# A two-layer attention kernel over an adjacency matrix: where in the loop the adjacency's byte blocks are made, when the projections' sums are taken, and in what order SyncE issues loads

## The chip, the cores and the metric

The kernel runs on one core of one Trainium2 chip. The metric is the device time of one execution in microseconds (us), given as the median of several runs. One further execution was recorded by the hardware profiler; the traces come from it. The engines are called PE (TensorE, matrix products), DVE (VectorE), ACT (ScalarE), POOL (GpSimd) and SP (SyncE, which here only issues DMAs).

## The reference

`x` is 3327 x 512, `adj` is 3327 x 3327 with zeros and ones (about 1% ones), `W_stack` holds two matrices of 512 x 1024 and `weight` is 512 x 512, all in float32.

```python
def gat_layer(x, W, adj):                      # twice, W = W_stack[0], W_stack[1]
    Wh, Ws = jnp.split(x @ W, 2, axis=-1)
    a = jax.nn.softmax(Wh @ Ws.T, axis=-1) * adj
    return jax.nn.leaky_relu(a @ Wh + x, 0.01)

y = gat_layer(gat_layer(x, W_stack[0], adj), W_stack[1], adj)
x = layernorm(x + y)
ba = jnp.maximum(jnp.sign(x), 0.0)             # zeros and ones
out = jax.nn.relu(adj @ (ba @ jnp.sign(weight).T))
return layernorm(x + out)
```

## The kernel before

**Tiles.** The 3327 rows are 26 row tiles of 128 (the last has 127). Two neighbouring tiles are a pair; there are 13 pairs (NQ). A pair of keys is called q, a pair of queries g; four row tiles are a chunk (7 chunks, the last of two tiles). Nearly every matrix product is done as seven block products instead of eight (the scheme of Strassen and Winograd), so each product needs sums of blocks before it and sums of results behind it. `left_sums` (L179 to L183) and `right_sums` (L185 to L189) are four DVE instructions each, and so their lines L180 to L189 show up in the profile for many tiles; `seven` (L144) is the chain of the seven products with the sums behind them (L162 on DVE, L159 on ACT).

**project(l)** (L233) prepares layer l. It loads the rows of x, transposes them chunk by chunk (`transpose_x`, L245; PE transposes at L253, tile pxt, copied to xT by `copy_out`, L119, which gives odd numbers to ACT and even ones to DVE at L123). `project_values` computes Wh of a pair (tile wh, products at L326) from sums s of xT (`keys`) and of W (`wsum`, L278 to L283), and behind it the sums t of wh (`done`). `queries` computes the other factor: (x M) with M = W_0 W_1^T, its products at L382, from sums of M (`sums_m`, tile msum) and sums xt of xT (`sums` within `queries`); then the sums of its results gsp (`done`) and their stores. Everything goes to memory (xs_d, ws_d, gs_d) for the attention. The loop over the chunks (L417) interleaves by `weave` the queries of chunk c, the values of chunk c and the transposes of chunk c+1. For c > 0 the sums xt of chunk c stand at the head of chunk c's own list (L428), while the sums s stand at the head of its values.

**attention(l)** (L446) is one software pipeline over 169 steps (g, q), g outer. Iteration v (from -34 on) issues, with a position between 0 and 1 for each item and a sort of them (L876), which is the order on each engine:

- loads by SP: ws of step v+2 (three buffers), adj of step v+4 (tile of 128x512, 256 KB, four buffers), xs and gs of scores to come;
- step v+3: `shift` (L620) and `exponential` (L623, ACT);
- step v+2: `running` (sum of the exponentials, L631), `masked` (times adj, L636) and the sums of the masked block on POOL (`sums`, L673 to L676, tiles s and as);
- the scores of a step 30 further on (L477, with copies on ACT and sums on DVE; `maximum`, L547). There are none left when v passes 151. Once per chunk `column_max` folds the maxima (L571) and transposes them (L579);
- the value products of step v: 14 matmuls at L700 into acc;
- one item of `later`, at 0.7. This is the list that `finish(g)` returns at the end of a row g (13 steps): `norm`, `residual`, and in the last layer also `sign`, `turn` (transposes pbt, L788) and `linear` (L798). `fetch(i)` loads the rows that `residual(i)` adds; it has two buffers for each name.

**Byte blocks.** The last stage multiplies by adj again. For it, each adjacency tile is written once as seven blocks of 128x128 bytes (tile ab, float8) to adj_d. Layer l does so in the steps whose q has the parity of l (`s2[1] % L == l`, L862), from the adj tile that the step has loaded anyway: `halved` (two ACT copies, L644 and L645), `halved_sums` (four DVE instructions, L655), `exact` (L664, which tests that the tile holds only zeros and ones, and ends the use of the adj tile) and, an iteration later, `keep_blocks` (store by POOL). So layer 0 does 91 tiles and layer 1 does 78, spread evenly over the rows.

**The end.** In layer 0's last iterations `early` has loads, transposes and products for layer 1's W and M. In layer 1 `load_products(v)` (L912) loads xw (the results of `linear`), forms the right sums of xw (`product_sums`, from step 158 on) and loads the byte blocks (`load_aggregate`); `aggregate` (L959) and `finale` (L964) do the last product and the layernorm.

Which engine's order is whose: SP issues its DMAs in the program's order, and an issue that waits holds up all issues behind it. The adj tile of a step in the last column pair (q = 12) or the last row (g = 12) is zeroed first by POOL, as a whole (L602), and SP's load of it waits for that.

The function that decides which step makes blocks, and the list at the end of a row:

```python
if s2[1] % L == l:
    work += [(-0.1, lambda: halved(*s2)), (0.6, lambda: halved_sums(*s2)),
             (0.62, lambda: exact(*s2))]
    after.append((0.05, lambda s2=s2: keep_blocks(*s2)))
...
fetch(0)
fetch(0)
if not last:
    return [norm, lambda: (residual(0), fetch(1)), lambda: None, lambda: residual(1)]
```

Of the kernel before, what the change touches and what calls it, by code (L numbers as in the profile page):

```python
# [9 lines left out]
F32 = mybir.dt.float32  # L10
# [9 lines left out]
P = 128  # L20
CT = 4
CW = CT * P
HW = CW // 2
# [6 lines left out]
def kernel(  # L30
# [8 lines left out]
    nc = tc.nc  # L39
    N, D = x.shape  # L40
    L = w_stack.shape[0]
# [7 lines left out]
    def rows(t):  # L49
        return min(P, N - t * P)  # L50
# [68 lines left out]
    def copy_out(n, dst, src):  # L119
        if n % 2:  # L120
            nc.scalar.copy(dst, src)
        else:
            nc.vector.tensor_copy(dst, src)  # L123
# [74 lines left out]
            do()  # L198

    ch_lane, acc_lane, tr_lane = (ps_ch, "ch"), (ps_acc, "acc"), (ps_tr, "tr")  # L200
    w_rows, wT, m_of = {}, {}, {}

    def load_w(l, h):

# [4 lines left out]
    def transpose_w(l, h, k, lane):  # L209
        pool, tag = lane  # L210
        pt = pool.tile([P, D], F32, tag=tag, name=f"pwT_{l}_{h}_{k}")
        for d in range(KD):
            nc.tensor.transpose(pt[:, ts(d, P)], w_rows[l, h, d][:, ts(k, P)], ident)
        wT[l, h, k] = slot([P, D], F32, f"wTs_{l}_{h}_{k}")
        copy_out(k, wT[l, h, k], pt)

    def product_m(l, lane):

# [14 lines left out]
    def project(l, pre):  # L233
# [11 lines left out]
        def transpose_x(c, k, lane):  # L245
            if k == 0:
                xTs[c] = pre.tile([P, KD, CW], F32, tag="xT", bufs=2, name=f"xT_{l}_{c}")
            pool, tag = lane
            pt = pool.tile([P, CW], F32, tag=tag, name=f"pxt_{l}_{c}_{k}")
            w = 0  # L250
            for a, t in enumerate(tiles_of(c)):
                r = rows(t)
                nc.tensor.transpose(  # L253
                    pt[:, w : w + r], rows_of[c][a][:r, ts(k, P)], ident[:r, :r]
                )
                w += r
            copy_out(k, xTs[c][:, k, :w], pt[:, :w])
            n = len(tiles_of(c)) * P
            if w < n:
                nc.gpsimd.memset(xTs[c][:, k, w:n], 0.0)  # L260
# [13 lines left out]
        if l == 0:  # L274
            for h in range(2):
                for k in range(KD):
                    transpose_w(l, h, k, (acc_lane, ch_lane)[h])
        wsum = ops.tile([P, 4, 2, HD], F32, tag="gs", name=f"wsum_{l}")  # L278
        lo, hi = wa[:, 0:2], wa[:, 2:4]
        right_sums(  # L280
            lo[:, :, :HD], lo[:, :, HD:], hi[:, :, :HD], hi[:, :, HD:],
            *(wsum[:, i] for i in range(4)),
        )  # L283
        wr = {B11: lo[:, :, :HD], B21: hi[:, :, :HD], B22: hi[:, :, HD:]}
        wr.update({i: wsum[:, e] for e, i in enumerate((T1, T2, T3, T4))})
        m = pre.tile([P, KD, D], F32, tag="m", bufs=1, name=f"m_{l}")
# [117 lines left out]
                for e in range(2):  # L404
                    nc.scalar.copy(m[:, 2 * e : 2 * e + 2], m_of[l][e])

        begin, *chains = queries(0, (ch_lane, acc_lane))
        if l == 0:
            first, second = (project_values(0, a, ch_lane) for a in range(2))
            weave(product_m(l, acc_lane), first + second, [begin])  # L410
            sums_m()
        else:
            first, second = (
                project_values(0, a, lane) for a, lane in enumerate((ch_lane, acc_lane))
            )
            weave(first, second, [sums_m, begin])
        for c in range(NC):  # L417
            turns = []
            if c + 1 < NC:
                turns = [lambda k=k: transpose_x(c + 1, k, tr_lane) for k in range(KD)]  # L420
            if c + 2 < NC:
                load_x(c + 2)
            if c == 0:
                weave(*chains, turns)
            else:
                start, one, two = queries(c, (ch_lane, ch_lane))
                if start:
                    one.insert(0, start)  # L428
                pairs = []
                for a in range(len(tiles_of(c)) // 2):  # L430
                    pairs += project_values(c, a, acc_lane)
                weave(one + two, pairs, turns)
# [13 lines left out]
    def attention(l, att):  # L446
# [150 lines left out]
        def load_adj(g, q):  # L597
            i0, n = half_cols(g)
            at = att.tile([P, 2, HW], F32, tag="adj", bufs=4, name=f"adj_{l}_{g}_{q}")
            adj[g, q] = at  # L600
            if n < HW or rows(2 * q + 1) < P:
                nc.gpsimd.memset(at, 0.0)  # L602
            if rows(2 * q + 1) == P:
                nc.sync.dma_start(
                    out=at[:, :, :n],
                    in_=adjT[2 * q * P : (2 * q + 2) * P, i0 : i0 + n].rearrange(
                        "(a p) i -> p a i", p=P
                    ),
                )
# [126 lines left out]
        def finish(g):  # L736
# [71 lines left out]
            fetch(0)  # L808
            fetch(0)
            if not last:  # L810
                return [norm, lambda: (residual(0), fetch(1)), lambda: None, lambda: residual(1)]
            return [
                norm, lambda: (residual(0), fetch(1)), lambda: sign(0), lambda: turn(0),
                lambda: linear(0), lambda: residual(1), lambda: sign(1), lambda: turn(1),
                lambda: linear(1),
            ]
# [1 line left out]
        if last:  # L818
            binary_weights()
        else:  # L820

            end = len(ahead) - LOOK
            early = {}
            for h in range(2):
                early[end - 14 + 2 * h] = [(0.9, lambda h=h: load_w(l + 1, h))]
                for k in range(KD):
                    early[end - 6 + KD * h + k] = [
                        (0.75, lambda h=h, k=k: transpose_w(l + 1, h, k, tr_lane))
                    ]
# [12 lines left out]
        later, after = [], []  # L842
        for v in range(-LOOK - 4, len(steps)):
            u = v + LOOK

            if 0 <= v + WS - 1 < len(steps):
                load_ws(*steps[v + WS - 1])
            if 0 <= v + 4 < len(steps):
                load_adj(*steps[v + 4])
            for lead, load in ((2, load_xs), (4, load_gs)):  # L850
                if 0 <= u + lead < len(ahead):
                    c, q, h = ahead[u + lead]
                    if h == 0 and (lead == 2 or q == 0):
                        load(c, q)
            work, after = after, []
            if 0 <= v + 3 < len(steps):
                s3 = steps[v + 3]
                work += [(0.0, lambda: shift(*s3)), (0.12, lambda: exponential(*s3))]
            if 0 <= v + 2 < len(steps):
                s2 = steps[v + 2]  # L860
                work += [(0.01, lambda: running(*s2)), (0.4, lambda: masked(*s2))]
                if s2[1] % L == l:  # L862
                    work += [
                        (-0.1, lambda: halved(*s2)), (0.6, lambda: halved_sums(*s2)),
                        (0.62, lambda: exact(*s2)),
                    ]
                    after.append((0.05, lambda s2=s2: keep_blocks(*s2)))
# [12 lines left out]
            if last:  # L880
                load_products(v)
# [30 lines left out]
    def load_products(v):  # L912
# [11 lines left out]
        for t in range(2 * NQ - 2):  # L924
            g, i = divmod(t, 2)
            made = (g + 1) * NQ - 1 + (5, 9)[i]
            if v == max(made + 1, first[t // XH] + t % XH):
                nc.sync.dma_start(out=xw[t], in_=xw_d[t])
        p = v - NQ * (NQ - 1) - 2
        if 0 <= p < EARLY:  # L930
            product_sums(p)
        if v == NQ * NQ - 1:
            product_sums(EARLY)
        n = v - NQ * NQ + 3 * NS
        if 0 <= n < 3 * NS:
            load_aggregate(*divmod(n, NS))
# [27 lines left out]
    def finale(att):  # L964
# [183 lines left out]
```

## Time and profile before

| what | value |
| --- | --- |
| median of 3 runs | 2673.2 us (2670.78 to 2673.9) |
| profiled execution, whole | 2675.18 us |
| its span (first to last instruction) | 2673.3 us |
| PE clock granted, mean | 0.996 of full |
| busy in the span | PE 98%, PE weight load 85%, DVE 78%, POOL 42%, ACT 30% |
| moved by DMA | 635.22 MB, mean 238 GB/s |
| steady row of 13 steps | 79.2 us (layer 0), 81.6 us (layer 1) |
| layer 0 to layer 1: last value product, first step of layer 1 | 1256.8 us, 1532.4 us |
| last row of layer 1 | 2463.9 to 2526.3 us |

A matmul of 128x128 by 128x256 follows the one before it every 0.216 us when nothing is late, though its row in the profile shows some 0.38 us for one, as they overlap in the pipeline. Rows of the timeline have the start, the length, the engine, the line, the operation with its output and inputs, the count, and in square brackets the idle time before it with what ended that. In the list of waits a line has the waiting engine, tile and line, the one waited for, and then the time in total, the number of times and the longest. "L700 PE ... acc" are the value products of the attention, "L477" the scores, "L326" and "L382" the projections, "L959" the last stage.

### The profile page before, as it was taken

How to read it: one execution, taken by the hardware profiler on the slowest of the kernel's cores; microseconds unless marked ns; L12 is line 12 of the kernel's file. 1: busy time of each engine (PE TensorE's matmuls, PEld its weight loads, DVE VectorE, ACT ScalarE, POOL GpSimd, SP SyncE). 2: the span in 40 equal slices, each digit the busy share in tenths (PEclk: the TensorE clock that was granted, in tenths of full speed). 3: DMA queues.
4: the chain of work that ended last, by engine and by line, in shares of the span. 5: the costliest groups of instructions: out<-in, count | busy, mean ns of one | idle time of the engine just before them, and what ended most of it. 6: DMA issues, size and time to landing. Idle time of an engine off the chain costs nothing. (4 is left out here: it accounts for less than half of the span.)

```text
span 2673.3 us, 40191 instructions
## 1 busy us (share of the span) xinstructions
PE 2621.3 (98%) x12839; PEld 2274.0 (85%) x12864; DVE 2075.2 (78%) x4227; ACT 797.9 (30%) x1976; POOL 1127.0 (42%) x2010
## 2 busy tenths in 40 slices
PE   9999999999999999999999999999999999999898
PEld 7888888888888888887888888888888888888687
DVE  5664788788888878888664578888888788889976
ACT  2333322222222222222332323232333323322142
POOL 2550344444444444657453044444444444456510
PEclk9999999999999999999999999999999999999999
DMA  5754767677776766877755667777777777687874
GB/s 195 262 205 155 249 230 258 229 255 236 263 236 230 256 226 234 274 251 232 272 201 190 216 208 267 244 239 248 243 267 238 248 253 237 235 275 264 268 247 167
DMA packets 276536, 635.22 MB, mean 238 GB/s; under 512 B 31809, under 2 KB 133031, under 8 KB 274782
## 3 DMA queue, kind: packets, MB, share of 16 engines
q1 hardware_dynamic: 240558, 526.13, 58.9%
q0 software_dynamic: 35760, 106.45, 11.0%
q8 instruction: 105, 1.72, 0.3%
q14 instruction: 113, 0.93, 0.1%
HBM read 525.52 MB, written 106.93 MB: 237 GB/s over the span
## 5 line engine op out<-in xcount | busy, mean ns | idle before, releaser
L477 PE MATMUL pZ<-gs,xs 128*128 128x256 f32 x2496 | 635.6, 379 | 0.0
L673 POOL TENSOR_TENSOR as<-s 128x128 f32<-128x128 f32 x338 | 159.4, 472 | 1008.7 <-DVE s L636 613.0
L477 PEld LDWEIGHTS pZ<-gs,xs 128*128 128x128 f32 x2496 | 473.7, 190 | 64.5
L700 PE MATMUL acc<-ws,s 128*128 128x256 f32 x1352 | 404.0, 380 | 0.0
L700 PE MATMUL acc<-ws,as 128*128 128x256 f32 x1352 | 351.2, 381 | 9.0 <-DMA ws<-ws_d 5.0
L700 PE MATMUL acc<-wh,s 128*128 128x256 f32 x1352 | 356.7, 380 | 0.3 <-DVE s L636 0.3
L477 PE MATMUL pY<-gs,xs 128*128 128x256 f32 x1248 | 320.3, 379 | 0.0
L623 ACT ACTIVATE s<-s 128x512 f32<-128x512 f32 x338 | 213.4, 631 | 294.9 <-DVE s L620 293.1
L700 PEld LDWEIGHTS acc<-ws,as 128*128 128x128 f32 x1352 | 255.4, 190 | 50.8 <-issue 9.6
L700 PEld LDWEIGHTS acc<-wh,s 128*128 128x128 f32 x1352 | 257.7, 191 | 36.1 <-DVE s L636 0.7
L700 PEld LDWEIGHTS acc<-ws,s 128*128 128x128 f32 x1352 | 256.9, 191 | 35.1 <-DVE h L732 0.5
L547 DVE TENSOR_TENSOR top<-top,s 128x512 f32<-128x512 f32 x312 | 225.5, 732 | 55.0 <-ACT s L529 36.6
L477 PEld LDWEIGHTS pY<-gs,xs 128*128 128x128 f32 x1248 | 237.0, 190 | 32.3
L620 DVE TENSOR_TENSOR s<-s,off 128x512 f32<-128x512 f32 x338 | 255.1, 755 | 0.1
L636 DVE TENSOR_TENSOR s<-s,adj 128x512 f32<-128x512 f32 x338 | 235.4, 696 | 8.6
L519 DVE TENSOR_TENSOR s<-p,u 128x256 f32<-128x256 f32 x156 | 67.2, 431 | 221.7 <-ACT u L494 221.7
L494 ACT COPY u<-pZ 128x256 f32<-128x256 f32 x312 | 116.2, 373 | 391.6 <-PE pZ L477 391.3
L631 DVE TENSOR_TENSOR total<-total,s 128x512 f32<-128x512 f32 x312 | 231.8, 743 | 0.0
L674 POOL TENSOR_TENSOR s<-s 128x128 f32<-128x128 f32 x338 | 201.6, 597 | 27.7
L675 POOL TENSOR_TENSOR as<-s 128x128 f32<-128x128 f32 x338 | 199.3, 590 | 26.5
L676 POOL TENSOR_TENSOR as<-s,as 128x128 f32<-128x128 f32 x338 | 193.4, 572 | 26.5
L700 PE MATMUL acc<-wh,as 128*128 128x256 f32 x676 | 203.4, 383 | 0.0
(200 smaller groups left out, 3914.7 us busy)
## 6 DMA issues: line engine op xcount, KB each, us to landing
ws<-ws_d SPq DMA_DIRECT2D x338, 512.0 KB, 3.8
xs<-xs_d SPq DMA_DIRECT2D x182, 512.0 KB, 5.8
adj<-in_adjT_dram SPq DMA_DIRECT2D x288, 256.0 KB, 4.3
xs<-xs_d SPq DMA_DIRECT2D x156, 384.0 KB, 6.3
gs_d<-gsp POOLq DMA_DIRECT2D x88, 256.0 KB, 3.2
gs<-gs_d SPq DMA_DIRECT2D x12, 1792.0 KB, 10.1
adj_d<-ab POOLq DMA_DIRECT2D x169, 112.0 KB, 3.3
ahl<-adj_d SPq DMA_DIRECT2D x78, 224.0 KB, 4.7
```

What stands on the lines that cost most here:

```text
L477: nc.tensor.matmul(ch[bank], xs[c, q, a][:, k], gs[c][:, b, k], start=(start and k == 0), stop=(k == 1), skip_group_check=True,)
L494: nc.scalar.copy(ch[name], ch[bank])
L547: nc.vector.tensor_tensor(top[i], top[i], t, ALU.max)
L620: nc.vector.tensor_tensor(s, s, off[g].to_broadcast([P, 2, HW]), ALU.subtract)
L623: nc.scalar.activation(sc[g, q], sc[g, q], AF.Exp)
L631: nc.vector.tensor_tensor(total[g], total[g], sc[g, q], ALU.add)
L636: nc.vector.tensor_tensor(s, s, adj[g, q], ALU.mult)
L673: nc.gpsimd.tensor_tensor(s3, a11, a21, ALU.subtract)
L674: nc.gpsimd.tensor_tensor(a21, a21, a22, ALU.add)
L675: nc.gpsimd.tensor_tensor(s2, a21, a11, ALU.subtract)
L676: nc.gpsimd.tensor_tensor(s4, a12, s2, ALU.subtract)
L700: nc.tensor.matmul(acc[g][i // 2][:, i % 2], a[i], b[i], start=(q == 0 and i % 2 == 0), stop=(q == NQ - 1), skip_group_check=True,)
```

## The change

Five things are changed.

1. **Byte blocks.** The tiles that belong to steps of the last four rows (step index 117 and up: 28 tiles in layer 0, 24 in layer 1) are made earlier, in steps of index below 117 whose q has the other parity, spread evenly over these ("room"). Such a step loads the late step's adj tile in addition to its own, with the same four buffers, and then does halved, halved_sums, exact and keep_blocks on it. The last four rows make no blocks.
2. **W's sums.** `wsum` of layer 1 is formed by `sums_w` in halves at steps 150 and 151 of layer 0's attention, not in project(1). In layer 0 it is formed at its old place, in halves (eight instructions for four).
3. **Projections.** The copies of pxt to xT for c > 0 are all on ACT. `prepare(c + 1)` makes the sums xt of chunk c+1 as the last item of chunk c's transposes, no longer at the head of chunk c+1's list.
4. **Loads.** `fetch(1)` goes into the next item of `later`. The adj tiles of the last row and column pair are zeroed only where the load leaves them free: the last column, or the second half of the tile. The loads of xw come two steps later.
5. **Sums of xw.** `product_sums(11)`, in the last iteration before, is done in `finale`, just ahead of `product_sums(12)`.

```diff
+    def sums_w(l, k):
+        if k == 0:
+            wsum_of[l] = ops.tile([P, 4, 2, HD], F32, tag="gs", name=f"wsum_{l}")
+        lo, hi = w_rows[l, 0, k], w_rows[l, 0, 2 + k]
+        right_sums(
+            lo[:, :HD], lo[:, HD:], hi[:, :HD], hi[:, HD:],
+            *(wsum_of[l][:, i, k] for i in range(4)),
+        )
...
-            copy_out(k, xTs[c][:, k, :w], pt[:, :w])
+            if c:
+                nc.scalar.copy(xTs[c][:, k, :w], pt[:, :w])
+            else:
+                copy_out(k, xTs[c][:, k, :w], pt[:, :w])
...
-        wsum = ops.tile([P, 4, 2, HD], F32, tag="gs", name=f"wsum_{l}")
+        if l == 0:
+            for k in range(2):
+                sums_w(l, k)
+        wsum = wsum_of[l]
         lo, hi = wa[:, 0:2], wa[:, 2:4]
-        right_sums(
-            lo[:, :, :HD], lo[:, :, HD:], hi[:, :, :HD], hi[:, :, HD:],
-            *(wsum[:, i] for i in range(4)),
-        )
...
+        def prepare(c):
+            start, *chains[c] = queries(c, (ch_lane, ch_lane if c else acc_lane))
+            if start:
+                start()
...
                 turns = [lambda k=k: transpose_x(c + 1, k, tr_lane) for k in range(KD)]
+                turns.append(lambda: prepare(c + 1))
...
-                start, one, two = queries(c, (ch_lane, ch_lane))
-                if start:
-                    one.insert(0, start)
+                one, two = chains[c]
...
-            if n < HW or rows(2 * q + 1) < P:
-                nc.gpsimd.memset(at, 0.0)
+            if n < HW:
+                nc.gpsimd.memset(at[:, :, n:], 0.0)
+            if rows(2 * q + 1) < P:
+                nc.gpsimd.memset(at[:, 1], 0.0)
...
             if not last:
-                return [norm, lambda: (residual(0), fetch(1)), lambda: None, lambda: residual(1)]
+                return [norm, lambda: residual(0), lambda: fetch(1), lambda: None,
+                        lambda: residual(1)]
             return [
-                norm, lambda: (residual(0), fetch(1)), lambda: sign(0), lambda: turn(0),
+                norm, lambda: residual(0), lambda: (sign(0), fetch(1)), lambda: turn(0),
                 lambda: linear(0), lambda: residual(1), lambda: sign(1), lambda: turn(1),
...
+            for k in range(2):
+                early[end - 2 + k].append((0.8, lambda k=k: sums_w(l + 1, k)))
...
+        first = NQ * (NQ - 4)
+        mine = [i for i, e in enumerate(steps) if e[1] % L == l]
+        room = [i for i, e in enumerate(steps[:first]) if e[1] % L != l][2:]
+        late = [i for i in mine if i >= first]
+        blocks = {i: steps[i] for i in mine if i < first}
+        blocks.update(
+            {room[n * len(room) // len(late)]: steps[i] for n, i in enumerate(late)}
+        )
...
                 load_adj(*steps[v + 4])
+                if blocks.get(v + 4, steps[v + 4]) != steps[v + 4]:
+                    load_adj(*blocks[v + 4])
...
-                if s2[1] % L == l:
+                of = blocks.get(v + 2)
+                if of:
...
-            if v == max(made + 1, first[t // XH] + t % XH):
+            if v == max(made + 3, first[t // XH] + t % XH):
...
-        if v == NQ * NQ - 1:
-            product_sums(EARLY)
...
-        product_sums(NQ - 1)
+        for p in range(EARLY, NQ):
+            product_sums(p)
```

More of the change, by code (lines that the diff above doesn't have):

```diff
@@ L200 @@
     ch_lane, acc_lane, tr_lane = (ps_ch, "ch"), (ps_acc, "acc"), (ps_tr, "tr")
-    w_rows, wT, m_of = {}, {}, {}
+    w_rows, wT, m_of, wsum_of = {}, {}, {}, {}
     def load_w(l, h):
@@ L405, in sums_m @@
                     nc.scalar.copy(m[:, 2 * e : 2 * e + 2], m_of[l][e])
-        begin, *chains = queries(0, (ch_lane, acc_lane))
+        chains = {}
+        def prepare(c):
+            start, *chains[c] = queries(c, (ch_lane, ch_lane if c else acc_lane))
+            if start:
+                start()
         if l == 0:
             first, second = (project_values(0, a, ch_lane) for a in range(2))
-            weave(product_m(l, acc_lane), first + second, [begin])
+            weave(product_m(l, acc_lane), first + second, [lambda: prepare(0)])
             sums_m()
@@ L415, in project @@
             )
-            weave(first, second, [sums_m, begin])
+            weave(first, second, [sums_m, lambda: prepare(0)])
         for c in range(NC):
@@ L423, in project @@
             if c == 0:
-                weave(*chains, turns)
+                weave(*chains[c], turns)
             else:
-                start, one, two = queries(c, (ch_lane, ch_lane))
-                if start:
-                    one.insert(0, start)
+                one, two = chains[c]
                 pairs = []
@@ L861, in attention @@
                 work += [(0.01, lambda: running(*s2)), (0.4, lambda: masked(*s2))]
-                if s2[1] % L == l:
+                of = blocks.get(v + 2)
+                if of:
                     work += [
-                        (-0.1, lambda: halved(*s2)), (0.6, lambda: halved_sums(*s2)),
-                        (0.62, lambda: exact(*s2)),
+                        (-0.1, lambda: halved(*of)), (0.6, lambda: halved_sums(*of)),
+                        (0.62, lambda: exact(*of)),
                     ]
-                    after.append((0.05, lambda s2=s2: keep_blocks(*s2)))
+                    after.append((0.05, lambda of=of: keep_blocks(*of)))
             if later:
```

## The prediction

> **What bounds the kernel now.** I read the first lines of the page, then the busy time by stretches of 100 us, then what PE waited for, then single stretches in order of time.
>
> ```profile
> span 2673.3 us, 40191 instructions
> ...
> PE   9999999999999999999999999999999999999898
> ...
> DVE  5664788788888878888664578888888788889976
> ```
>
> PE is busy in 98% of the span, so it sets the end, and only stretches in which it isn't full can give time back. The stretches show where:
>
> ```profile
> 700.00:800.00 100.00, 100.00 (x470) 88.02 (x469) 84.74 (x171) 29.78 (x77) 43.91 (x79) 1.00 0.74 252
> 1200.00:1300.00 100.00, 91.93 (x402) 72.76 (x401) 84.67 (x167) 24.52 (x56) 60.02 (x100) 0.98 0.68 230
> 2400.00:2500.00 100.00, 91.30 (x419) 76.58 (x420) 94.89 (x184) 25.41 (x59) 63.20 (x109) 0.98 0.83 280
> 2500.00:2600.00 100.00, 93.02 (x736) 80.47 (x739) 80.11 (x201) 33.40 (x64) 24.62 (x44) 0.97 0.70 235
> ```
>
> The columns are the stretch, its length, busy time of PE, PE's weight load, DVE, ACT and POOL, PE's clock, the DMA share and GB/s. From 700 to 800 us PE never rests, though DVE is busy in 85%. At the layer boundary (1200 to 1300) and the end of the last attention layer (2400 to 2530) it loses some 8 us per 100, and the clock falls below 1. What it waited for:
>
> ```profile
> PE pbt L788 <- DVE ba L782: 5.1, 1, 5.1
> PE acc L700 <- DMA ws<-ws_d: 5.0, 2, 4.4
> PE pxt L253 <- DVE xT L123: 3.4, 1, 3.4
> PE pZ_g L382 <- ACT h_wh L159: 2.9, 6, 0.5
> PE pZ_wh L326 <- DVE s L181: 2.7, 2, 2.3
> PE acc L700 <- POOL s L674: 2.7, 1, 2.7
> ```
>
> (microseconds in total, times, longest). Each is few and long: they are events, not a steady loss. Three cost more than they show, because PE ran at half clock after them:
>
> ```profile
> 1284.39 0.66 PE L253 MATMUL pxt<-ident,xr 128*128 128x128 f32 x4 [3.37 <-DVE xT L123]
> 1284.89 3.44 PE L382 MATMUL pY_g<-xt,msum 128*128 128x256 f32 x8
> ```
>
> Eight such matmuls took 1.89 us at 1276.91. After the gap of 3.37 they took 3.44; after the gaps of 4.38 (2474.56) and 5.14 (2499.24), pairs took 0.86 instead of 0.43. After gaps of 2.35 (1263.09) and 2.70 (2464.91) nothing slowed. So a gap between 2.70 and 3.37 or above costs about 1.6 to 2.6 us more than its length. [...]
>
> **Part 1: blocks (halved, halved_sums, exact) moved out of the last rows.** A block costs DVE 2.36 us (2444.52 to 2446.88: four L655 of 0.28 to 0.54, one L664 of 0.83, 0.08 for its accumulator), ACT 0.71 and POOL 0.56. The last row of layer 1 lasts 62.4 us (2463.9 to 2526.3). PE's work in it is 41.8: 13 steps of 14 matmuls at 0.216, 3.02 each, plus 2.5 for transposes and finish(11). In the stretches 2489.2 to 2498.6 and 2510.7 to 2521 PE does run 3.02 a step, so that is attainable. The excess of 20.6 is waits (2.70 + 4.38 + 0.59 + 5.14 + 0.33 + 0.79 = 13.9), about 5 of half clock, and small ones. DVE is busy 59.8 of the 62.4. Without five to six blocks (-11.4 measured between 2468.75 and 2521.9, up to -14 for six) and with one product_sums (1.04) gone to the finale, DVE has about 45 left beside PE's 41.8. So DVE, not PE, sets this row: 45 to 48 us. That takes off 14 to 17; I take **-16** for the row with the ws waits of part 4, bounds -12 (ws still late) and -20.6 (PE alone).
>
> In layer 0 the last rows have DVE 0.88 busy and PE waits of 0.63, 0.85 and 0.54 (1190, 1206, 1234) within 3.9 us of excess: **-3** (-1.5 to -4).
>
> What it adds: 28 and 24 blocks in the first nine rows, two to four per row, each between two steps that have blocks of their own, and each with its own load of adj. DVE's steady rows (79.2 us in layer 0, 81.6 in layer 1) hold 64 to 68.2 us; three blocks add 7.1, so the share goes from 0.81-0.84 to 0.90-0.93. Below 1, with about 10 us from a mask product to the matmul that needs it, an extra 2.36 is absorbed. Two covers are thin: the fold L571 ends 0.22 us before its transposes in layer 0's rows (once per two rows), and POOL's sums have 4 to 7 us. If a block falls just before a fold, PE waits up to 2.36. I take **+1.5** (0 to +6, a wait of half a block at five of twelve folds). The loads are 52 x 256 KB, 13.3 MB over 1500 us, 9 GB/s beside 252; a load lands in 4.3 us and is issued four steps (24 us) early, but the same four buffers hold fewer steps ahead; the buffer comes free when the exactness test of the iteration before ends, which leaves about 0.9 of an iteration of 6.1 us. Hidden, at zero; without the cover the step's mask product would wait, inside DVE's 10 us.
>
> [...] In the trace 128x512 sums of two SBUF inputs took 0.68 where POOL ran no sums (L186 to L189, 1261.41 to 1264.4) and 0.69 to 0.76 on average where POOL is busy 0.44. [...]
>
> **Part 2: W's sums earlier (sums_w), copies of xT to ACT, xt sums a chunk sooner (prepare).** At the boundary, PE's wait of 2.35 for s (L181) is DVE being late through the four wsum (L186 to L189, 1261.41 to 1264.4); they go to steps 150 and 151, where DVE has room, so that s is ready 2.4 sooner. But the xt sums behind hang on msum, which stands in DVE's order behind neg_w, whose DMA lands at 1269.9 in either order: most of what is won there is waited again. The gap of 3.37 is the copy L123 at 1283.65, queued on DVE behind t's sums; on ACT (30% busy) it is done when the transposes end. That gives 3.37 and the 1.6 of half clock, and I take 0.8 of the rest: **-5.8** (-4 to -7). Layer 0's start has eight half sums for four whole: **+0.2**.
>
> The chunks behave otherwise. Now, chunk starts 2 to 5 of each layer cost PE 0.48 to 0.69 (the wait for ACT's h_wh), against 0 where nothing is late; from start to start 0.63 more than the matmuls. DVE's order there is t (four, 1.47), s (four), xt (four, 2.53), and PE's first product needs only s. After the change, prepare(c+1) stands at the end of the chunk before, so DVE does xt (2.53) first, then the queries' sums gs (L189 at 1320.59 is the last of four, 2.52), then t (1.47), then s up to L181 (0.87). From the last value sum wb (L162, 0.35 apart from the next): 0.35 + 2.53 + 2.52 + 1.47 + 0.87 = 7.74, and about 0.14 to PE (1265.29 to 1265.44 at the boundary): 7.88. PE's product for wb began 1.06 before that sum (1330.08 and 1331.14); from there to the product that needs s it has eight groups of four matmuls (0.8625 each) and four transposes (0.436): 6.9 + 0.436 - 1.06 = 6.28. It waits 1.60 at L326 where it lost 0.63: 0.97 x 8 = **+7.7**. Bounds: -5 (0.63 x 8) if s comes in time, +10 if ACT's h_wh follows late as well.
>
> **Part 3: loads moved on SyncE.** fetch(1) goes one item later. At 2359.75 PE waits 1.56 for xs, since SP's issue of it stood from 2345.24 to 2352.80 behind fetch(1), which waits for residual(0): **-1.7** (0 to -2). Past it move the ws, adj and xs loads of one iteration; it is itself needed two or three items later, 12 us or more, and lands in 4.
>
> **Part 4: memset only where needed, xw loads two steps later.** In the last row, SP waits:
>
> ```profile
> SPq L604 <- POOL adj L602: 14.7, 7, 3.9
> ...
> SPq L681 <- PE acc L700: 10.3, 8, 3.4
> SPq L115 <- DMA xres<-x_d: 8.2, 3, 3.6
> ```
>
> The 14.7 is adj's load behind POOL's memset, and the ws load behind it is the 4.38 gap. The memset of 128x512 (0.53 x 10) becomes a column or a half tile. The wait goes; next late is the fetch, called twice, on the same queue (8.2), two to four us a time, and ws has three buffers of 3 us. This is inside the -16 above. The xw loads are used by product_sums from step 158 on, and only tiles 22 and 23 come later for it (part 5): zero.
>
> **Part 5: product_sums(11) into the finale.** Its 1.04 now stands before product_sums(12), which PE's wait of 1.2 for L187 shows to be on the path at that point: **+1.0** (0 to +1.1).
>
> **Sum**: -16 - 3 + 1.5 - 5.8 + 0.2 + 7.7 - 1.7 + 1.0 = -16.1. From the profiled execution's 2675.18 that gives 2659.1. That execution lies 2.0 above the median of 2673.2, so **2657 us**.
>
> **Rivals.**
> A (13%, the other side): the first 117 steps pay for the blocks. Mechanism: a block in DVE's queue delays fold, or the mask product before a value step, past PE's need. It decides against the gain from 16.1/52 = 0.31 us per moved block on; at 0.6 each (a quarter of a block) it is +31, less the +1.5 counted: 2657 + 30 = 2687. For: fold's cover of 0.22, DVE to 0.93. Against: no PE wait between 700 and 800 with DVE at 0.85, and 10 us of slack.
> B (18%): the chunk starts don't wait, as the sums in front of s were never late by as much as the order says. Then +7.7 becomes about -3: 2646.
> C (17%): the last row stays bound by ws behind the double fetch, or DVE finds no pace: half the gain, -8: 2665.
> D (5%): the change does not do what it says at all, the waits return elsewhere in the same size: 2670 to 2676.
> My forecast (47%): 2652 to 2662.
>
> **How the numbers follow.** Range 2642 to 2670 takes in the forecast, B, C and a part of D, and leaves out A and tails. Some 0.2% (5.3 us, 2667.9 to 2678.5) is what a measurement of this kernel tells from no change. Faster by more: forecast, B and 0.14 of C, 0.79. Within: D, 0.03 of C and 0.02 of A, 0.10. Slower: the other 0.11 of A.
>
> **What would show it.** Right: the last row (L700 to the first L959) at 45 to 48 us with no half clock in it; no PE wait on xT at the second chunk of layer 1; PE waits of about 1.6 for s (L181's) at the starts of chunks 2 to 5; steady rows still 79.2 and 81.6. Wrong: rows of the first nine that are longer by 1 us or more, with waits of ptop for top or acc for s; chunk starts below 0.6; a last row above 54 us.

## The result, and the profile after

The changed kernel takes **2681.4 us** (median of 10 runs, 2679.74 to 2685.08) against 2672.69 us (10 runs, 2670.78 to 2673.95) before: a ratio of 1.0035 with a 95% interval of 1.0026 to 1.0045. It is slower by a third of a per cent, where 2657 was forecast, with a range of 2642 to 2670. The profiled execution took 2681.87, its span is 2680.1.

The page of the changed kernel has nearly the same first lines:

```profile
span 2680.1 us, 40370 instructions
...
PE   9999999999999999999999999999999999999897
...
DVE  5554888899888996666755488988899888767876
```

DVE's digits are higher in the middle of each attention layer and lower at its end: the blocks were moved as the change says. The stretches of 100 us (columns as before) show where time came and went:

```profile
400.00:500.00 100.00, 95.71 (x436) 83.45 (x435) 85.74 (x183) 29.67 (x79) 39.63 (x78) 0.97 0.72 246
500.00:600.00 100.00, 100.00 (x468) 88.02 (x467) 89.17 (x189) 30.96 (x82) 42.74 (x82) 1.00 0.77 265
...
700.00:800.00 100.00, 96.28 (x438) 83.89 (x437) 85.79 (x184) 29.04 (x78) 39.16 (x77) 0.97 0.73 244
...
1200.00:1300.00 100.00, 96.95 (x435) 77.69 (x434) 73.77 (x132) 24.05 (x47) 55.65 (x102) 1.00 0.69 227
...
2400.00:2500.00 100.00, 94.91 (x447) 81.17 (x449) 72.49 (x121) 22.16 (x43) 56.97 (x104) 1.00 0.81 274
```

The boundary (1200 to 1300) and the end (2400 to 2500) gained, as forecast. These stretches don't hold quite the same work (the last row begins at 2463.9 before and at 2479.7 here); the table further down compares like with like. But PE, which was full from 300 to 1000 us, now loses about 4 us in two of these stretches, with a lowered clock, while the stretch between them, with DVE at 89%, is full. What PE waited for:

```profile
PE pZ_wh L338 <- DVE s L181: 12.3, 9, 1.7
PE pZ L494 <- ACT u L511: 9.7, 5, 4.3
...
PE acc L719 <- DMA ws<-ws_d: 4.6, 3, 3.7
PE agg L992 <- DVE wh L187: 2.0, 2, 1.5
```

Eight of the nine waits in the first line are the chunk starts, forecast at 1.60 each. The second is new and was not forecast: scores (L494) that wait for a copy on ACT (L511). On PE it looks like this, in the seventh step of layer 0's row 1:

```profile
414.23 0.59 PE L719 MATMUL acc<-ws,s 128*128 128x256 f32 x2
419.12 2.08 PE L494 MATMUL pZ<-gs,xs 128*128 128x256 f32 x4 [4.29 <-ACT u L511]
420.99 1.06 PE L719 MATMUL acc<-wh,as 128*128 128x256 f32 x2
```

and on ACT:

```profile
418.20 0.40 ACT L663 CAST ab<-adj 128x256 fp8e4<-128x256 f32 x1 [7.22 <-DMA adj_d<-ab]
418.51 0.29 ACT L664 CAST ab<-adj 128x128 fp8e4<-128x128 f32 x1
418.71 0.36 ACT L511 COPY u<-pZ 128x256 f32<-128x256 f32 x1
```

ACT stood 7.22 us in front of `halved`, the cast into the block tile ab, because ab has two buffers and the store of the block two before (adj_d<-ab) had not landed. Behind it in ACT's order stood the copy u that PE needed. PE's 4.29 is followed by half clock: two matmuls take 1.06 instead of 0.59. POOL had issued that store at 407.05, right behind one of a residual:

```profile
406.50 0.56 POOL L115 DMA_DIRECT2D x_d<-h  x1 [2.84 <-DVE h L786]
407.05 0.54 POOL L677 DMA_DIRECT2D adj_d<-ab  x1
```

It took 11.1 us to land, the longest of the 169 stores of ab:

```profile
DMA to landing us min/median/max: 2.0/3.9/11.1
```

Before, the longest took 7.3, and ACT never waited for one.

The time of a row (13 steps, from its first value matmul to the next row's first, and for a layer's last row to the end of its last value matmul) adds it up:

| stretch, us | before | after | difference | forecast |
| --- | --- | --- | --- | --- |
| rows 0 to 8 of layer 0 | 712.8 | 727.4 | +14.6 (row 1 +7.4, row 5 +7.0) | +1.5 for both layers |
| rows 0 to 8 of layer 1 | 731.6 | 736.1 | +4.5 (rows 1, 4, 5, 8) | (in the line above) |
| rows 9 to 12 of layer 0 | 251.7 | 249.8 | -1.9 | -3 |
| rows 10 and 11 of layer 1 | 124.4 | 122.2 | -2.2 | -1.7 |
| last row of layer 1 | 62.4 | 51.7 | -10.7 | -16 |
| to layer 0's first row | 292.4 | 296.2 | +3.8 | +0.2 and half of +7.7 |
| layer 0's end to layer 1's first row | 275.6 | 272.6 | -3.0 | -5.8 and half of +7.7 |
| behind the last row | 147.0 | 148.7 | +1.7 | +1.0 |

The differences are +6.8 in sum, which is 2680.1 - 2673.3.

### The profile page after: what moved, and what is told of

Its sections match the earlier page's. It is cut to its first block, busy times and chain, and to the rows that moved or that the text cites. A ratio compares the mean times of both kernels' runs of the same rounds, so it can differ in the third digit from the quotient of the medians.

```text
span 2680.1 us, 40370 instructions
## 1 busy us (share of the span) xinstructions
PE 2622.6 (98%) x12839; PEld 2273.6 (85%) x12864; DVE 2059.8 (77%) x4211; ACT 813.0 (30%) x2000; POOL 1093.4 (41%) x2029
## 2 busy tenths in 40 slices
DMA packets 290800, 648.84 MB, mean 242 GB/s; under 512 B 32765, under 2 KB 147295, under 8 KB 289046
## 5 line engine op out<-in xcount | busy, mean ns | idle before, releaser
L494 PE MATMUL pZ<-gs,xs 128*128 128x256 f32 x2496 | 640.3, 381 | 10.9 <-ACT u L511 9.7
L692 POOL TENSOR_TENSOR as<-s 128x128 f32<-128x128 f32 x338 | 163.9, 485 | 1011.1 <-DVE s L655 661.3
L494 PEld LDWEIGHTS pZ<-gs,xs 128*128 128x128 f32 x2496 | 475.1, 191 | 79.6 <-ACT u L511 12.8
L494 PE MATMUL pY<-gs,xs 128*128 128x256 f32 x1248 | 320.3, 379 | 0.0
L494 PEld LDWEIGHTS pY<-gs,xs 128*128 128x128 f32 x1248 | 237.0, 190 | 32.3
L639 DVE TENSOR_TENSOR s<-s,off 128x512 f32<-128x512 f32 x338 | 247.9, 734 | 0.1
L511 ACT COPY u<-pZ 128x256 f32<-128x256 f32 x312 | 116.1, 372 | 328.8 <-PE pZ L494 328.2
L694 POOL TENSOR_TENSOR as<-s 128x128 f32<-128x128 f32 x338 | 205.1, 607 | 26.5
L693 POOL TENSOR_TENSOR s<-s 128x128 f32<-128x128 f32 x338 | 182.2, 539 | 27.7
L695 POOL TENSOR_TENSOR as<-s,as 128x128 f32<-128x128 f32 x338 | 179.4, 531 | 26.5
## 6 DMA issues: line engine op xcount, KB each, us to landing
gs<-gs_d SPq DMA_DIRECT2D x12, 1792.0 KB, 10.5
```

The lines of the kernel that those rows point to most:

```text
L494: nc.tensor.matmul(ch[bank], xs[c, q, a][:, k], gs[c][:, b, k], start=(start and k == 0), stop=(k == 1), skip_group_check=True,)
L511: nc.scalar.copy(ch[name], ch[bank])
L639: nc.vector.tensor_tensor(s, s, off[g].to_broadcast([P, 2, HW]), ALU.subtract)
L692: nc.gpsimd.tensor_tensor(s3, a11, a21, ALU.subtract)
L693: nc.gpsimd.tensor_tensor(a21, a21, a22, ALU.add)
L694: nc.gpsimd.tensor_tensor(s2, a21, a11, ALU.subtract)
```

## The experiments

Eleven kernels. Medians of before in the same sets of runs were 2672.86, 2671.95 and 2673.97 us (first four, next four, last three).

**1. A third buffer for ab in layer 0.**

```diff
-            t = att.tile([P, 7, P], F8, tag="adj_b", bufs=2, name=f"ab_{g}_{q}")
+            t = att.tile([P, 7, P], F8, tag="adj_b", bufs=3 - l, name=f"ab_{g}_{q}")
```

> A third buffer for the byte-block tile ab in layer 0's attention only (there is no room for it in layer 1's, which serves as the control). Theory R (ring): a block in the step between two others leaves the third of three only 0.85 of a step to get its buffer back, and the store of the first lands later than that; ACT waits, and PE behind it. Then rows 1 and 5 of layer 0 go from 86.6 and 86.2 us to 79.2, the half clock after them goes, layer 1's rows stay as in the changed kernel (82.2, 82.9, 82.5 and 83.2 in rows 1, 4, 5 and 8): 2681 - 14.4 = 2667 (2665 to 2669). Theory Q (DVE's queue: the block's 2.36 us of DVE are what is late): nothing moves, 2681. Theory L (the added loads crowd the transfers): nothing moves, 2681.

Measured: 2669.86 us, ratio 0.9987 (0.9978 to 0.9997), just above what was expected. Rows 1 and 5 of layer 0 are 79.2 and 79.3; layer 1's rows 1, 4 and 8 are 82.1, 83.5 and 83.2 still. Row 5 of layer 1 is 81.6, without a change to it, and 81.5 in runs 2 to 5: its 82.5 was seen in the changed kernel's trace alone. ACT's cast no longer waits there:

```profile
411.03 0.37 ACT L511 COPY p<-pY 128x256 f32<-128x256 f32 x1 [1.35 <-PE pY L494]
411.30 0.41 ACT L663 CAST ab<-adj 128x256 fp8e4<-128x256 f32 x1
411.60 0.30 ACT L664 CAST ab<-adj 128x128 fp8e4<-128x128 f32 x1
412.32 0.37 ACT L511 COPY u<-pZ 128x256 f32<-128x256 f32 x1 [0.42 <-PE pZ L494]
```

Theory R holds: with the same blocks on DVE and the same loads, one buffer takes 14.3 us off the rows 0 to 8 of layer 0 (727.4 to 713.1). The stores are no faster, the longest takes 11.3; ACT no longer waits for them. The median falls by 11.5 only, as other stretches of this trace are longer by 1.8 in sum. That alone turns the change from slower to slightly faster than before. That layer 1 has no room for a third buffer was not shown: no run tries it there.

**2. The added loads left out.**

```diff
-                    load_adj(*blocks[v + 4])
+                    adj[blocks[v + 4]] = adj[steps[v + 4]]
```

> The changed kernel without the 52 added loads of adj: a moved block is made from the tile that its step has loaded for itself, so the byte blocks of the moved steps hold other data and the last product is of other numbers; all else is the same. Theory R (ring): the stores still have to land within 0.85 of a step, so rows 1 and 5 of layer 0 stay near 86 us or lose at most a few us of it, 2676 to 2682. Theory L (the added 13.3 MB of loads make the stores late): the waits for ab go in both layers, 2681 - 19 = 2662. Theory Q: unchanged, 2681.

Measured: 2678.4 us, ratio 1.0023 (1.0013 to 1.0032). Rows 1 and 5 stay at 84.7 and 86.5, and ACT waits for ab as before (32.3 us in 12 waits, against 29.9 in 10):

```profile
418.56 1.13 PE L494 MATMUL pZ<-gs,xs 128*128 128x256 f32 x4 [3.56 <-ACT u L511]
```

Theory L falls: the 13.6 MB of added loads (648.84 MB are moved in the changed kernel, 635.21 here) cost at most some 3 us.

**3. Sums s ahead of sums xt.** `prepare(c)` calls `keys` of the chunk's first pair first:

```diff
         def prepare(c):
+            if c:
+                sums_of[c, 0] = keys(c, 0)
             start, *chains[c] = queries(c, (ch_lane, ch_lane if c else acc_lane))
...
```

> The changed kernel, with the sums s of the next chunk's first pair ahead of the sums xt at the end of each chunk (keys, then prepare). Theory O (order of sums on DVE): s is late only because xt, gs and t stand ahead of it, so the eight waits of 1.45 to 1.66 at the starts of chunks 2 to 5 go, and xt is still in time (4.4 us of DVE against 6.3 of PE): 8 x 1.60 = 12.8 less, 2668.5 (2667 to 2671); if the old loss of 0.63 comes back it is 2673.6. Theory C (the xT copies, all four on ACT now, hold the chunk start): the waits stay, 2681.

Measured: 2665.28 us, ratio 0.9964 (0.9952 to 0.9977), in its trace 15.2 us less than the changed kernel (2664.9 against 2680.1). That is more than was expected: the eight waits were 12.0 in sum, and the two projections are 6.8 and 7.0 us shorter. In the changed kernel DVE's order at a chunk start is xt, gs, t and then s:

```profile
1331.10 0.68 DVE L186 TENSOR_TENSOR gsp<-b,gsp 128x512 f32<-128x512 f32 x1
...
1335.55 0.42 DVE L181 TENSOR_TENSOR s<-s,xT 128x256 f32<-128x256 f32 x1
```

and PE's product waits for that s:

```profile
1336.12 1.10 PE L338 MATMUL pZ_wh<-wsum,s 128*128 128x256 f32 x4 [1.45 <-DVE s L181]
```

With keys first the same product (now L340) follows without a gap:

```profile
1326.85 0.60 PE L263 MATMUL pxt<-ident,xr 128*128 128x128 f32 x4
1327.29 1.03 PE L340 MATMUL pZ_wh<-wsum,s 128*128 128x256 f32 x4
```

Theory O holds; neither the 1.60 nor the old 0.63 is left at any of the eight starts.

**4. xt back at the head of its chunk.**

```diff
-                turns.append(lambda: prepare(c + 1))
...
-                one, two = chains[c]
+                start, one, two = queries(c, (ch_lane, ch_lane))
+                if start:
+                    one.insert(0, start)
```

> The changed kernel with the sums xt of each chunk back at the head of its own list, as before; the copies to xT stay on ACT. Theory O: each of the eight chunk starts goes from 1.60 back to about 0.63, or less as the DVE copy of xT is gone: -7.8, 2673.5 (2671 to 2675). Theory C (copies on ACT): the waits stay, 2681.

Measured: 2673.29 us, ratio 0.9997 (0.9987 to 1.0006). The waits of 1.45 to 1.66 are the old ones again (0.47 to 0.69), with the copies to xT still on ACT. Between 80 and 180 us PE waited for:

```profile
PE pZ_g L394 <- ACT h_wh L159: 1.4, 3, 0.5
PE pZ_g L394 <- DVE xt L187: 0.7, 1, 0.7
```

The median is 8.1 us below the changed kernel's (2681.4 - 2673.3). In the trace the two projections give 3.7 and 2.5 of this: in layer 1 PE now waits 2.06 for xt at the boundary, where it waited 0.45. So the loss at the chunk starts comes from the place of `prepare`, and none of it from the copies.

**5. One fetch(0).**

```diff
             fetch(0)
-            fetch(0)
```

> The changed kernel with fetch(0) called once instead of twice. Theory S (SyncE's queue): in the last row of layer 1 the second fetch stands on SP until the first has landed (8.1 us in three waits), the ws loads behind it come late, and that is PE's wait of 3.70 (and 0.37, 0.57) for ws. Then these go and the last row falls from 51.7 to 47 to 48 us: 2677 (2676 to 2678). Theory D (DVE, busy 0.94 of this row, sets it): the wait for ws goes and others for DVE's or POOL's sums take its place, the row stays at 50.5 to 51.7, 2680.5 to 2681.5.

Measured: 2679.06 us, ratio 1.0024 (1.0015 to 1.0034). The wait for ws is gone from the last row, and others took its place. In it PE waited for:

```profile
PE pbt L807 <- DVE ba L801: 4.1, 2, 2.9
PE acc L719 <- POOL as L694: 1.2, 2, 0.8
PE pz L767 <- POOL adj L619: 0.9, 1, 0.9
```

The row is 50.9 instead of 51.7, as theory D said: S falls, D holds for the row. The median lies between the two forecasts, 2.3 us below the changed kernel's; most of the trace's gain is outside the row, in the stretch behind it (146.5 instead of 148.7) and in rows 0 to 8.

**6. Layer 1 without moved blocks at q 4 and 8.**

```diff
-        room = [i for i, e in enumerate(steps[:first]) if e[1] % L != l][2:]
+        room = [i for i, e in enumerate(steps[:first]) if e[1] % L != l and (l == 0 or e[1] not in (4, 8))][2:]
```

> The changed kernel; in layer 1 the moved blocks do not go to steps with q 4 or 8, in layer 0 nothing is different. Theory H: of the blocks that stand third of three, those pay in layer 1 whose first one's store is queued on POOL right behind the 256 KB store of h (residual(0), residual(1)), which are these. Then rows 1, 4, 5 and 8 of layer 1 go from 82.2, 82.9, 82.5 and 83.2 to 81.5 or 81.6: -4.5, 2677 (2676 to 2678), and layer 0's rows 1 and 5 stay near 86. Rival: which store is late is a matter of where the gs loads and others fall, and the waits move to other rows in the same sum, 2681.

Measured: 2681.48 us, ratio 1.0031 (1.002 to 1.0043). ACT's waits for ab are gone from layer 1 (14.9 us in 4, all in layer 0), as theory H said. The time is not: rows 1, 4, 5 and 8 are 82.9, 82.6, 81.5 and 82.6. Two other waits are there. In rows 4 and 8, with a moved block at q 2, PE waits for u (0.66 each; the changed kernel has these two as well, 0.66 and 0.67). In row 4:

```profile
1890.25 1.13 PE L494 MATMUL pZ<-gs,xs 128*128 128x256 f32 x4 [0.66 <-ACT u L511]
```

and ACT had waited for DVE's shift (L639), which stood behind a block, two maxima and a residual:

```profile
1889.31 0.63 ACT L642 ACTIVATE s<-s 128x512 f32<-128x512 f32 x1 [4.87 <-DVE s L639]
1889.85 0.35 ACT L511 COPY u<-pZ 128x256 f32<-128x256 f32 x1
```

In row 1, now with blocks at q 12 and at q 0 of the next row (four in succession), PE waits for xs, whose load SP issued late:

```profile
1695.20 1.10 PE L494 MATMUL pZ<-gs,xs 128*128 128x256 f32 x4 [1.10 <-DMA xs<-xs_d]
```

H named the right waits on ACT, but they held only a part of layer 1's price, and the new places brought the wait for xs. The new theory, that q 2 and the succession 12, 0 cost, is tried in 9.

**7. Blocks not moved, all else of the change kept.**

```diff
-        blocks = {i: steps[i] for i in mine if i < first}
-        blocks.update(
-            {room[n * len(room) // len(late)]: steps[i] for n, i in enumerate(late)}
-        )
+        blocks = {i: steps[i] for i in mine}
```

> The changed kernel with part 1 undone: each layer makes the blocks of its own parity in their own steps, nothing is loaded twice; all the rest of the change stays. Theory B: moving the blocks is what freed DVE in the last rows, so the last row of layer 1 goes from 51.7 back to 59 to 61 us, rows 9 to 11 lose some 2 more, and the rows before them are 79.2 and 81.6 throughout: 2681.4 - 18.9 + 11 = 2673.5 (2671 to 2676). Rival M (the smaller memset alone shortened the last row): it stays near 52, 2664.

Measured: 2676.97 us, ratio 1.0018 (1.0008 to 1.0027), a little above what was expected. All rows 1 to 8 are 79.2 and 81.5 to 81.6; the last row of layer 1 is 61.6, with

```profile
PE pbt L807 <- DVE ba L801: 8.5, 2, 5.6
PE acc L719 <- POOL as L694: 4.3, 4, 2.6
```

So theory B holds: the smaller memset and the fetch bring 0.8 us of the last row (62.4 to 61.6), the moved blocks 9.9 (61.6 to 51.7). What was not expected is row 11 of layer 0 at 66.4, against 63.0 before: there `sums_w` stands on DVE ahead of a fold, and PE waits 2.56 for it; with the blocks moved away it is 0.80.

**8. All repairs.** Third buffer (1), keys first (3), one fetch (5), the room of (6), and

```diff
-        constants()
         for p in range(EARLY, NQ):
             product_sums(p)
+        constants()
```

> All that the theories R, O, S and H ask for: a third buffer of ab in layer 0, keys of the next chunk's first pair ahead of xt, one fetch(0), no moved block at q 4 or 8 of layer 1; and product_sums(11) and (12) before the constants of the last stage instead of behind them. If each of them is right and they add up: 2681.4 - 14 (ab) - 15 (sums) - 4 (fetch) - 4.5 (room) - 1.5 (product sums, which wait 6.67 us for ACT's square root now) = 2642 (2639 to 2647). If the fetch gives nothing (theory D): 2646. If the ring's waits come back elsewhere: 2655 or above.

Measured: 2646.91 us, ratio 0.9905 (0.9889 to 0.9922), near the 2646 of the case in which the fetch gives nothing. The terms of that sum were not as expected: `room` gave nothing in run 6 where 4.5 was put, and the stretch behind the last row is 143.9 instead of 148.7, -4.8 where 1.5 was put; the two misses cancel by luck. The measured parts do add up: by runs 1, 3, 5 and 6 the first four repairs are -11.5, -16.1, -2.3 and +0.1, which with -4.8 makes 2646.8. The -4.8 was not run by itself: that stretch is about 144 in runs 8 to 10, and between 146.5 and 151.0 in the other traces.

**9. The same, layer 1's moved blocks at q 0, 6 and 10 only.**

```diff
-        room = [i for i, e in enumerate(steps[:first]) if e[1] % L != l and (l == 0 or e[1] not in (4, 8))][2:]
+        room = [i for i, e in enumerate(steps[:first]) if e[1] % L != l and (l == 0 or e[1] in (0, 6, 10))][2:]
```

> As the run with all repairs, but layer 1's moved blocks go to q 0, 6 and 10 only. Theory: what is left of part 1's price in layer 1 (83.3, 82.6 and 82.6 in rows 1, 4 and 8, against 81.5 and 81.6) has two causes: a moved block at q 2, whose 2.36 us of DVE stand beside residual's 2.2 and make the exponential late, which stands ahead of a score copy on ACT (0.66 at PE); and blocks at q 12 and then q 0, four in succession, which hold an xs load on SP behind an adj load without a buffer (1.5 at PE). Neither is left then: -3.6, 2643.5 (2642 to 2645). If these waits come with the number of blocks and not with their places, they move, 2647.

Measured: **2643.8 us**, ratio 0.9888 (0.9871 to 0.9904), the fastest version. Rows 1, 4, 5 and 8 of layer 1 are 81.5, 81.6, 81.5 and 81.6: the price of moved blocks in layer 1 was one of places. Which of the places left out (q 2, the succession of 12 and 0) brought how much is read from run 6's waits alone. Its longest waits that are left:

```profile
PE pxt L263 <- DMA xr<-in_x_dram: 5.1, 3, 4.0
PE pbt L811 <- DVE ba L805: 4.2, 2, 2.9
PE acc L723 <- POOL as L698: 2.1, 4, 0.8
```

**10. The repairs of 8, no block moved.** The diffs of 3, 5, 7 and 8's last together.

> As the run with all repairs, but no block is moved (each in its own step, as before). Theory B: moved blocks are worth what the last rows show, 10 in the last row of layer 1 and 2 to 4 in layer 0's, and cost nothing once their waits are gone, so this is 2647 + 9 to 12 = 2656 to 2659. Rival: with the sums, the fetch and the product sums in order, the last row is short in any case, 2647 to 2650.

Measured: 2658.49 us, ratio 0.9943 (0.9926 to 0.9959). The last row is 61.7 again, row 11 of layer 0 65.6. Moving the blocks is worth 14.7 us (2658.5 - 2643.8) once its waits are gone.

**11. The last row without sums of xw.** With one fetch, `product_sums` of the loop is left out and the last product reads columns of xw instead.

```diff
         if 0 <= p < EARLY:
-            product_sums(p)
+            a = min(2 * p % XH, XH - 3)
+            xt[p] = xw_tiles[2 * p // XH][:, a : a + 2].rearrange("p a (b n) -> p (a b) n", n=HD)
```

> The changed kernel with one fetch(0) and without the eleven product_sums of the loop: the last product reads other numbers in their place, so its result is not the sums' product; all else is done. It takes 10 x 1.6 us of DVE out of the last row of layer 1. Theory D (DVE sets the last row): the row goes from 50.9 (run with one fetch) to 43 to 46 us, close to PE's own 41.8, and pbt's waits for ba (4.1) and acc's for POOL's sums go: 2679 - 6 = 2673 (2671 to 2675). Rival (loads or the order of steps set it): it stays at 49 to 51, 2678 to 2679.

Measured: 2674.29 us, ratio 0.9999 (0.999 to 1.0009). The last row falls from 50.9 to 46.3, a little above the expected 43 to 46. The row in the changed kernel and here:

```profile
2479.70:2531.40 51.70, 43.78 (x201) 35.18 (x203) 48.49 (x96) 8.75 (x15) 35.47 (x65) 1.00 0.85 295
```

```profile
2477.80:2524.20 46.40, 42.75 (x201) 35.69 (x203) 37.46 (x57) 8.79 (x15) 35.37 (x65) 1.00 0.91 315
```

DVE's time goes from 48.5 to 37.5, and PE follows: theory D holds for this row. The ten product_sums had taken 16.1; DVE gains less, as what else it does takes 37.5 in the shorter row, with POOL busy 0.76 of it, instead of 48.5 - 16.1 = 32.4 with POOL busy 0.69.

## Why the prediction was wrong

**The step that failed** is the one in part 1 on what the moved blocks add: "Below 1, with about 10 us from a mask product to the matmul that needs it, an extra 2.36 is absorbed", taken at +1.5 with 0 to +6. It measured +19.1 (14.6 + 4.5). As far as it went, it was right: DVE at 0.91 and 0.92 in rows 3 and 4 of layer 0 cost nothing (79.2 and 79.4), and the loads were hidden but for some 3 us at most (run 2). It followed DVE, POOL, the loads and adj's four buffers, but not the other tile that a block goes through, ab, with two buffers that come free only when a store has landed. It even noted the fact that decides, that each moved block lies between two steps with blocks of their own, and drew nothing from it. The third of three needs the buffer of the first within about 0.85 of a step (5.2 us); the stores land in 3.9 us in the median, but in up to 11.1. In the place shown above ACT was ready for the third block at 410.98, 3.9 us behind the issue of the first one's store.

Runs 1 and 2 show that this is layer 0's 14 us. Why the two stores that stopped PE there took 11.1 and 10.5 us stays open: each was issued within 0.8 us behind a 1792 KB load of gs by SP and a store of a residual by POOL, and no run takes these away; without the added loads ACT still waited 6.5 and 6.9. Layer 1's 4.5 is shared: rows 4 and 8 are 82.6 in run 6, without any wait for ab, so that about 2.0 belongs to the late exponential at q 2; the other 2.5 has ACT's waits for ab in front of PE's (0.46, 0.73 and 0.32). Run 9's places avoid both.

**Rival A** ended near the result (2687) by another mechanism. DVE's queue did delay PE, but only at two places of layer 1, by 0.66 each; A's price of 0.6 for each of the 52 blocks was 31 us. That ACT, the least busy engine of the four that compute (30%), could be the one to hold PE was in none of the cases.

**The last row**: -16 was forecast, -10.7 measured, in the same mechanism. The mis-sized term is "DVE has about 45 left": it is 48.5. Of the sum's 59.8 - 11.4 (or 14) - 1.04 the last part was not in this row: before, too, the row held ten product_sums, and the one that went to the finale ran at 2527 to 2529, behind it. And the sums that stayed became longer: the ten product_sums take 16.1 instead of 14.9, a running sum 0.87 instead of 0.75. The wait for ws behind the double fetch was there (3.70), but run 5 shows that it stood in front of DVE's lateness.

**Layer 0's last rows**: -3 against -1.9; the sums of W at steps 150 and 151, costed at nothing, take part of it (row 11 at 66.4 in run 7).

**The chunk starts**: +7.7 forecast, and the waits are 1.45, 1.45, 1.45 and 1.66 in each layer, for old waits of 0.48 to 0.69. From one start to the next it is 27.61 us instead of 26.64: the +0.97 that DVE's order of instructions gave. Runs 3 and 4 show that it was the order alone. Rival B falls.

**The boundary**: -5.8 against -6.9 (-3.0 less the 3.9 of layer 1's chunk starts). PE's 3.37 and the half clock are gone. **SyncE's fetch(1)**: -1.7 against -1.8 (row 10 of layer 1, 66.2 to 64.4). Not all of it is sure to come from there: run 7, which keeps this part, has 65.7, with a wait of 0.99 for xs. **product_sums(11)**: +1.0 against +0.7 in PE's waits for L187 (1.24 to 1.97); the other 1.0 of that stretch lies partly behind the last matmul (13.4 us to the end against 12.8).

Without the failing step and with the right last row the sum is 2675.2 - 10.7 - 1.9 + 7.7 - 6.9 - 2.2 + 1.7 = 2662.9. That is an estimate of what the third buffer and better places, with nothing else, would have given; no run has just these.

## What to carry to other kernels

When work is moved to another step, list every rotating buffer that it passes through, with what releases each, and check the shortest distance between two uses, not the mean: here it was the tile that a store's landing releases, 3.9 us in the median and up to 11.1. A wait on ACT, idle 70% of the time, stopped PE, busy 98%, for 4.29 us, so a wait counts by what stands behind it. The order of sums that share an engine is a lever of its own: putting first what the next product needs gave 16 us here against the changed kernel's order and 8 against the old one (run 4), for no work less.

## What the runs showed of the hardware

**Half clock after a gap does not follow the gap's length alone.** In the changed kernel a gap of 3.70 was followed by full speed:

```profile
2491.80 1.10 PE L719 MATMUL acc<-ws,as 128*128 128x256 f32 x4 [3.70 <-DMA ws<-ws_d]
2492.74 0.59 PE L719 MATMUL acc<-ws,s 128*128 128x256 f32 x2
```

and in run 1 one of 2.10 by matmuls at half speed from a microsecond behind it on (four take 1.81 and 1.91 instead of 1.03):

```profile
2499.12 0.40 PE L807 MATMUL pbt<-ident_h,ba 128*128 128x128 bf16 x4 [2.10 <-DVE ba L801]
...
2500.27 1.81 PE L719 MATMUL acc<-wh,s 128*128 128x256 f32 x4
2501.88 1.91 PE L719 MATMUL acc<-ws,as 128*128 128x256 f32 x4
```

Gaps of 2.92 (run 8) and 2.93 (run 9) at the same instruction went both ways: behind the first, four matmuls took 1.91, behind the second 1.03. The prediction's threshold between 2.70 and 3.37 is therefore not one. In the traces of before and of the changed kernel, behind the first 20 us, half clock came within 2 us of the end of 5 of the 6 gaps of 3.3 and more, and of neither of the two gaps of 2.0 to 3.3 (2.35 and 2.70); the one left of the six is the 3.70. What else decides it, no run shows.

**In the changed kernel's trace a DVE sum that starts while one of POOL's runs ends after it.** The same sum of xw (128x256, f16) in the last row, with POOL busy 0.69, as a mean of ten (0.491 us), and in the last stage, where POOL runs no sum (0.29):

```profile
L187 DVE TENSOR_TENSOR wh<-xw,wh 128x256 f16<-128x256 f16 x10 | 4.9, 491 | 0.3
```

```profile
2550.26 0.29 DVE L187 TENSOR_TENSOR wh<-xw,wh 128x256 f16<-128x256 f16 x1
```

The mean hides two lengths. Two sums of the same line in the last row, and the sum on POOL beside the second:

```profile
2495.79 0.28 DVE L189 TENSOR_TENSOR wh<-xw,wh 128x256 f16<-128x256 f16 x1
2498.93 0.54 DVE L189 TENSOR_TENSOR wh<-xw,wh 128x256 f16<-128x256 f16 x1
2498.73 0.58 POOL L693 TENSOR_TENSOR s<-s 128x128 f32<-128x128 f32 x1
```

Of the 52 sums of xw in this trace, 21 start while a sum runs on POOL. They take 0.43 to 0.54, and each ends 0.15 us after POOL's sum does. The other 31 take 0.28 to 0.29, also the 13 of them in whose time POOL starts a sum. The running sums (128x512, f32) do the same: 71 of 312 start while a sum runs on POOL, take 0.94 or more and end 0.54 to 0.55 after it; the others take 0.68 to 0.69. That a DVE sum that starts second waits for POOL's to end is read from this order of the starts and ends alone; no run here took POOL's work away by itself. The sums that stayed in the last row became longer: a running sum takes 0.87 there instead of 0.75, with POOL busy 0.69 of the row instead of 0.66.
